# One token sum a slot later, and the last softmax sum taken by TensorE from an unaccumulated unit

## The chip, the cores and the metric

One Trainium2 chip, one core. The metric is device time in microseconds, the median of several executions; lower is better. A profile of one execution of each kernel is at hand.

## What is computed

A transformer block with conditioned norms, in float32, on `x` of shape (4, 1024, 512) with 16 heads of width 32 and a hidden layer of 2048. Cut to what matters:

```python
def norm(x, t, gw, gb, bw, bb):
    g, b = (t @ gw.T + gb)[:, None, :], (t @ bw.T + bb)[:, None, :]
    return g * x * rsqrt(mean(x * x, -1) + 1e-6) + b

def attention(x):                     # q, k, v are projections of x, per head
    p = softmax(einsum('blhd,bmhd->bhlm', q, k) / sqrt(dh))
    return einsum('bhlm,bmhd->blhd', p, v).reshape(B, L, D) @ Wo.T

def swiglu(x):
    return silu(x @ gate_w.T) * (x @ hid_w.T) @ out_w.T

y = x + attention(norm(x, t, g1...))
out = x + y + swiglu(norm(y, t, g2...))
```

## The kernel before

**Tiles.** Activations lie with the features on the partitions. The 4096 tokens are 8 blocks (`n`) of 512; the 512 features are 4 groups (`hg`) of 4 heads. Attention goes by token groups `j` (64 in all: block, head group and half of 256 queries), and each group is 4 units (`r`, 256 in all) of 256 keys. A unit is one tile `raw[r]` of 128 keys x 2 x 4 heads x 256 queries, 1024 KB, from a pool of 10.

**One unit.** `scores` (TensorE, L337), `keep` (ScalarE copies them to `raw`, L344), `running_max` (VectorE, L349), `shifted` (VectorE subtracts the group's maximum, L390), `exponential` (ScalarE, L393), `weighted` (TensorE, `av`, L403) and `accumulate` (L417). The last one gathers the denominators: units 1 to 3 of a group are added into unit 0 by an accumulating DMA that GpSimd (POOL) issues. Each waits for the one before it, since all write the same tile.

**One group.** `fold_sum` (VectorE, L425) adds the two halves of the accumulated tile; `sums` (TensorE, L435, tile `sum`) multiplies by ones to add over the partitions, 4 matmuls; `sums_out` (ScalarE, L440), `inverse` (VectorE, L443) and `normalize` (L452) follow.

**Slots.** The order of PE, DVE, ACT and POOL is written out by hand in a loop over slots `g`: slot `g` issues the scores of unit `g`, the exponential of unit `g - 5`, `av` and the accumulation of unit `g - 6`; every fourth slot (`kind` 0) issues the fold and sums of group `g // 4 - 3`. So the last accumulation (unit 255) stands in slot 261 and the last fold (group 63) in slot 264. SyncE's queue, which issues the plain loads and stores, is ordered by the framework.

**The hidden layer beside it.** From slot 60 on, each two slots also hold one step `p` (128 hidden features for one block, 16 steps per block). Gate and hidden products use a seven-product scheme in the manner of Strassen, on 2 x 2 halves of weights and of tokens. `token_sums(n, i)` makes the sums of token halves for block `n`, in four VectorE instructions on 128x512: T1 (`i = 0`, L518), T2 (`i = 1`, L520), an in-place difference T3 (`i = 2`, L522) and T4 (`i = 3`, L524). T1 is read by `pair_15`, T2 by the right half of `pair_26`, T3 by `pair_7`, T4 by `pair_4`. In an even slot the order around the change is:

```python
scores(g); fold_sum(j_n); shifted(r_x); weighted(r_v); accumulate(r_v); keep(g)
pair_26(p); copy_156(p); take_sums(j_n); exponential(r_x)   # take_sums: sums, sums_out
one(); two()                        # contraction of an earlier step, tile pc
pair_7(p); sub_5(p)
```

and in an odd one `scores`, `shifted`, `weighted`, `keep`, then `pair_3`, `pair_15` of the next step, `add_15` (L551), `gate` (L588), `pair_4` and `hidden` (L591). Work given to `after(g, ...)` is issued at the end of slot `g`. Block `n` begins its hidden layer at slot `g0 + 28`, `g0 = 32 (n + 1)`; that slot has kind 0. For the last block, n = 7, the token sums are issued by a loop of their own behind the slots.

The tiles `sum` and `pc` share a pool of two PSUM banks (tag `w`), and the contraction reads `ow`, 256 KB loaded by SyncE (`load_ow`, L595) a step ahead.

Of the kernel before, what the change touches and what calls it, by code (L numbers as in the profile page):

```python
# [24 lines left out]
def tile_cond_transformer_block(  # L25
# [13 lines left out]
    nc = tc.nc  # L39
# [7 lines left out]
    DH = D // N_HEADS  # L47
    HG = P // DH
# [3 lines left out]
    UN = KT // 2  # L52
# [19 lines left out]
    ones_sum = const.tile([P, DH], F32, tag="ones_sum", name="ones_sum")  # L72
# [45 lines left out]
    raw, rmax, shift, mT, av, acc, avs, oT = {}, {}, {}, {}, {}, {}, {}, {}  # L118
# [16 lines left out]
    def norm_squares(dst, tag: str, k: int):  # L135

        sq = [sb.tile([P, NB], F32, tag="t", name=f"sq{tag}_{2 * k + i}", bufs=2) for i in range(2)]
        for i in range(2):
            nc.scalar.activation(sq[i], dst[:, 2 * k + i, :], AF.Square)
        if k == 0:  # L140
            state[tag] = sb.tile([P, NB], F32, tag="tot", name=f"tot{tag}", bufs=1)
            nc.vector.tensor_tensor(state[tag], sq[0], sq[1], ALU.add)
        else:
            for t in sq:
                nc.vector.tensor_tensor(state[tag], state[tag], t, ALU.add)
# [53 lines left out]
    def norm_scale(dst, tag: str, c: int):  # L199
        nc.vector.tensor_tensor(dst[:, c, :], dst[:, c, :], state[tag], ALU.mult)  # L200

    def norm_mod(which: int, b: int, dst, c: int):
        nc.scalar.activation(  # L203
            dst[:, c, :],
            dst[:, c, :],
            AF.Identity,
            bias=mod[:, (2 * which + 1) * C + c, b : b + 1],
            scale=mod[:, 2 * which * C + c, b : b + 1],
        )
# [201 lines left out]
    def accumulate(r: int):  # L411

        j, u = divmod(r, UN)
        if u == 0:
            acc[j] = raw[r]
        else:
            nc.gpsimd.dma_start(  # L417
                out=acc[j].rearrange("p k h q -> p (k h q)"),
                in_=raw[r].rearrange("p k h q -> p (k h q)"),
                accum_op=ALU.add,  # L420
            )
# [9 lines left out]
    def sums(j: int):  # L431
        total = ps.tile([P, HQ], F32, tag="w", name=f"sum{j}")
        a = acc.pop(j)
        for i in range(HG):
            nc.tensor.matmul(total[i * DH : (i + 1) * DH, :], ones_sum, a[:, 0, i, :], start=True, stop=True)  # L435
        state["sum", j] = total

    def sums_out(j: int):
# [257 lines left out]
    NR = NBLK * C * (NB // HQ) * UN  # L696
# [11 lines left out]
    def pin(g, fn, *a):  # L708
        pinned.setdefault(g, []).append((fn, a))

    def between(g, fn, *a):
        halfway.setdefault(g, []).append((fn, a))

    def after(g, fn, *a):
        ended.setdefault(g, []).append((fn, a))
# [40 lines left out]
    for n in range(NBLK):  # L756
        g0 = (n + 1) * BS
        pin(g0 + 6, load_res, n)
        e = g0 if n == 0 else g0 - 4
        go = e + 13 if n < NBLK - 1 else g0 + 8  # L760
        for d in range(C):
            first.append((go, None, project_out, (n, d)))
            pin(go - 3 + (d // 2 * 4 if n else 0), load_wo, n, d)
        if n < NBLK - 1:
            tag = f"f{n}"
            after(e + 16, add_res, n)
            for k in range(2):
                after(e + 15 + k, lambda n=n, tag=tag, k=k: norm_squares(x2[n], tag, k))
            if n == 0:
                between(e + 17, norm_mean, tag, False)  # L770
            else:
                amid.setdefault(e + 17, []).append((norm_mean, (tag, True)))
            after(e + 17, norm_compact, tag)
            after(e + 19, take, tag)
            after(e + 21, root, tag)
            after(e + 22, invert, tag)
            after(e + 22, put, tag)
            after(e + (23 if n == 0 else 24), norm_spread, tag)
            scales, mods = ((24, 24, 25, 25), (25, 25, 26, 26)) if n == 0 else ((22, 22, 24, 24), (23, 23, 25, 25))
            for c in range(C):  # L780
                after(g0 + scales[c], lambda n=n, tag=tag, c=c: norm_scale(x2[n], tag, c))
                between(g0 + mods[c], lambda n=n, c=c: norm_mod(1, n // QB, x2[n], c))
            for i in range(4):
                after(g0 + (26, 26, 27, 28)[i] - (n > 0 and i == 0), token_sums, n, i)
    for m in range(NBLK * C):
        if m:
            for qh in range(NB // HQ):
# [24 lines left out]
    with tc.manual_schedule(  # L812
# [75 lines left out]
        def take_sums(j: int):  # L888

            if 0 <= j < NR // UN:  # L890
                sums(j)
                sums_out(j)
                if j >= direct:
                    inverse(j)
                    normalize(j)

        while g < END:
# [31 lines left out]
            if v_on:  # L929
                weighted(r_v)  # L930
                accumulate(r_v)
# [120 lines left out]
        n = NBLK - 1  # L1052
# [9 lines left out]
        for i in (1, 3):  # L1062
# [5 lines left out]
                start=True,  # L1068
                stop=True,
# [104 lines left out]
```

## Time and profile before

| | us |
|---|---|
| median of 3 runs | 2425.66 (2425.57 to 2426.95) |
| the profiled execution | 2425.87 |
| its span, first to last instruction | 2424.1 |
| TensorE busy in it | 2374.3 (98%) |
| VectorE busy | 1975.1 (81%) |
| ScalarE busy | 1420.1 (59%) |
| accumulating transfers of `raw` | 192 x 1024 KB, 9.2 median to landing |

Busy TensorE time counts pipelined matmuls by modelled ends. An engine's idle time matters only if another engine's work waits behind it. Times of the profiled execution are compared with its own 2425.87, not with the median.

### The profile page before, as it was taken

To read this page: it belongs to the slowest core of one execution; us is meant where nothing else is said; L and a number is where in the kernel's file an instruction comes from. 1 tells how busy PE (TensorE), PEld (TensorE's weight loads), DVE (VectorE), ACT (ScalarE), POOL (GpSimd) and SP (SyncE) were. 2 spreads that over 40 slices of the span, in tenths; PEclk is the share of its full clock that TensorE was granted. 3 is DMA by queue.
4 is the path that set the end of the run, shared out by engine and by line. 5 is a ranking of instruction groups with operands and counts; after the bars stand their busy time and mean duration, and the time that the engine had idled before them with its cause. 6 is when DMAs were issued, how large, how long until landed. Compare 5 with 4: busy or idle time off the path is not lost. (4 is left out here: it accounts for less than half of the span.)

```text
span 2424.1 us, 74021 instructions
## 1 busy us (share of the span) xinstructions
PE 2374.3 (98%) x33149; PEld 1153.2 (48%) x33149; DVE 1975.1 (81%) x2295; ACT 1420.1 (59%) x1519; POOL 172.4 (7%) x207
## 2 busy tenths in 40 slices
PE   9999999999999999999999999999999999989999
PEld 4333434345454544544454545454545454434665
DVE  2688888889799988998899979997999799835544
ACT  4677776766566656665576657665666576412111
POOL 0000000000000000000000000000000000000000
PEclk9999999999999999999999999999999999999999
DMA  6699999889888888889888888898887988862331
GB/s 226 188 295 254 262 251 241 222 220 239 199 203 212 204 226 199 216 212 229 196 211 217 221 201 213 202 238 202 206 210 197 231 197 219 209 213 82 126 106 53
DMA packets 184843, 499.79 MB, mean 206 GB/s; under 512 B 21191, under 2 KB 78535, under 8 KB 157134
## 3 DMA queue, kind: packets, MB, share of 16 engines
q0 software_dynamic: 28656, 208.68, 44.4%
q1 hardware_dynamic: 155582, 286.37, 35.0%
q8 instruction: 261, 4.28, 0.7%
q14 instruction: 56, 0.46, 0.1%
q10 hardware_dynamic: 288, 0.01, 0.0%
HBM read 244.34 MB, written 41.97 MB: 118 GB/s over the span
## 5 line engine op out<-in xcount | busy, mean ns | idle before, releaser
L390 DVE TENSOR_TENSOR raw<-raw,shift 128x2048 f32<-128x2048 f32 (+1 forms) x320 | 588.8, 1857 | 26.1 <-ACT shift L385 26.1
L344 ACT COPY raw<-sc 128x2048 f32<-128x2048 f32 x256 | 479.4, 1873 | 186.2 <-PE sc L337 127.8
L393 ACT ACTIVATE raw<-raw 128x2048 f32<-128x2048 f32 x256 | 490.7, 1917 | 147.5 <-DVE raw L390 145.3
L349 DVE TENSOR_TENSOR rmax<-rmax,raw 128x1024 f32<-128x1024 f32 x384 | 469.5, 1223 | 47.6 <-ACT raw L344 41.0
L113 PE MATMUL pc<-h,ow 128*32 128x512 f32 x3328 | 379.9, 595 | 2.5 <-ACT raw L393 1.5
L417 POOL DMA_DIRECT2D raw<-raw x192 | 165.3, 861 | 1940.7 <-ACT raw L393 839.0
L337 PE MATMUL sc<-q,k 32*128 32x256 f32 x4096 | 293.3, 400 | 0.8 <-ACT raw L344 0.8
L403 PE MATMUL av<-raw,v 128*32 128x256 f32 x4096 | 272.5, 384 | 21.3 <-ACT raw L393 20.8
L113 PE MATMUL pa<-x,fa 128*32 128x256 f32 x4096 | 270.0, 381 | 3.5 <-DVE pa L551 2.5
L113 PE MATMUL pa<-sums,fw 128*32 128x256 f32 x4096 | 267.9, 379 | 0.0
L337 PEld LDWEIGHTS sc<-q,k 32*128 32x128 f32 x4096 | 185.0, 184 | 117.1 <-issue 74.9
L113 PE MATMUL pkq<-y,wkq 128*32 128x512 f32 (+1 forms) x1664 | 230.8, 596 | 0.9 <-ACT y L203 0.7
L113 PEld LDWEIGHTS pc<-h,ow 128*32 128x32 f32 x3328 | 103.7, 110 | 206.9 <-issue 193.0
L113 PEld LDWEIGHTS pa<-x,fa 128*32 128x32 f32 x4096 | 123.3, 110 | 112.1 <-DVE pa L551 20.9
L113 PEld LDWEIGHTS pa<-sums,fw 128*32 128x32 f32 x4096 | 133.1, 110 | 87.9
L403 PEld LDWEIGHTS av<-raw,v 128*32 128x32 f32 x4096 | 110.6, 109 | 134.5 <-ACT raw L393 48.7
L113 PE MATMUL pb<-x,fw 128*32 128x256 f32 x2048 | 134.7, 379 | 1.2 <-ACT pb L566 1.2
L113 PE MATMUL pa<-x,fw 128*32 128x256 f32 x2048 | 134.0, 379 | 0.0
L113 PE MATMUL pb<-sums,fa 128*32 128x256 f32 x2048 | 133.9, 379 | 0.0
L583 ACT ACTIVATE t<-pa 128x512 f32<-128x512 f32 x128 | 78.3, 612 | 92.9 <-PE pa L113 92.6
L113 PEld LDWEIGHTS pkq<-y,wkq 128*32 128x32 f32 (+1 forms) x1664 | 72.6, 117 | 125.3 <-issue 117.4
L385 ACT COPY shift<-sp 128x512 f32<-128x512 f32 x128 | 75.0, 586 | 95.0 <-PE sp L113 95.0
(132 smaller groups left out, 2338.2 us busy)
## 6 DMA issues: line engine op xcount, KB each, us to landing
raw<-raw POOLq DMA_DIRECT2D x192, 1024.0 KB, 9.2
fw<-sw SPq DMA_DIRECT2D x128, 512.0 KB, 7.3
fa<-in_gh_w SPq DMA_DIRECT2D x128, 384.0 KB, 6.1
ow<-in_out_w SPq DMA_DIRECT2D x104, 256.0 KB, 3.6
wkq<-in_kq_w SPq DMA_DIRECT2D x32, 512.0 KB, 5.8
v<-vs SPq DMA_DIRECT2D x128, 128.0 KB, 6.4
k<-kqs SPq DMA_DIRECT2D x124, 128.0 KB, 6.8
kqs<-st SPq DMA_DIRECT2D x61, 256.0 KB, 8.0
```

The costliest lines, as they stand in the source:

```text
L113: nc.tensor.matmul(dst[k : k + n, :], w[:, k : k + n], moving, start=start, stop=stop, skip_group_check=seeded)
L337: nc.tensor.matmul(sc[:, i, k, :], keys[rows, k * P : (k + 1) * P], queries[rows, :], start=True, stop=True)
L344: nc.scalar.copy(raw[r].rearrange("p k h q -> p h k q"), state.pop(("sc", r)))
L349: nc.vector.tensor_tensor(rmax[j], rmax[j], raw[r][:, k, :, :], ALU.max)
L385: nc.scalar.copy(shift[j][:, k : k + 2, :], pp)
L390: nc.vector.tensor_tensor(t, t, s.unsqueeze(1).to_broadcast(list(t.shape)), ALU.add)
L393: nc.scalar.activation(raw[r], raw[r], AF.Exp)
L403: nc.tensor.matmul(av[j][i * DH : (i + 1) * DH, :], v[m, u][:, k, i * DH : (i + 1) * DH], raw[r][:, k, i, :], start=(kt == 0), stop=(kt == ...
L417: nc.gpsimd.dma_start(out=acc[j].rearrange("p k h q -> p (k h q)"), in_=raw[r].rearrange("p k h q -> p (k h q)"), accum_op=ALU.add,)
L583: nc.scalar.activation(state["t", p], bank_a[p], AF.Tanh, scale=0.5)
```

## The change

Two edits. In `accumulate`, the last unit of all (`r = 255`) is no longer added by a DMA; instead `sums` of its group issues its 4 ones-matmuls three times into the same PSUM tile, first on the folded tile, then on the two halves of `raw[255]` as they are. And T2 is issued at the end of slot `g0 + 27` instead of `g0 + 26` for the blocks n = 1 to 6, where it now stands behind that slot's VectorE work and directly ahead of T3. Block 0 keeps its order.

```diff
@@ accumulate
         if u == 0:
             acc[j] = raw[r]
-        else:
+        elif r < NR - 1:
             nc.gpsimd.dma_start(
                 out=acc[j].rearrange("p k h q -> p (k h q)"),
                 in_=raw[r].rearrange("p k h q -> p (k h q)"),
@@ sums
         a = acc.pop(j)
-        for i in range(HG):
-            nc.tensor.matmul(total[i * DH : (i + 1) * DH, :], ones_sum, a[:, 0, i, :], start=True, stop=True)
+        parts = [a[:, 0]]
+        if (j + 1) * UN == NR:
+            parts += [raw[NR - 1][:, k] for k in range(2)]
+        for k, part in enumerate(parts):
+            for i in range(HG):
+                nc.tensor.matmul(
+                    total[i * DH : (i + 1) * DH, :],
+                    ones_sum,
+                    part[:, i, :],
+                    start=(k == 0),
+                    stop=(k == len(parts) - 1),
+                )
         state["sum", j] = total
@@ the calendar
             for i in range(4):
-                after(g0 + (26, 26, 27, 28)[i] - (n > 0 and i == 0), token_sums, n, i)
+                after(g0 + ((26, 26, 27, 28) if n == 0 else (25, 27, 27, 28))[i], token_sums, n, i)
```

The order of all other instructions on every engine, and of SyncE's queue, is the same in both kernels.

## The prediction

> **What bounds the kernel now.** I read the page's engine shares first, then the waits, then the stretch of the timeline around each place that the change touches. TensorE is busy for 98% of the span, so an edit counts only where it moves the start of a matmul. The idle time at the two places:
>
> ```profile
> PE 2374.3 (98%) x33149; PEld 1153.2 (48%) x33149; DVE 1975.1 (81%) x2295; ACT 1420.1 (59%) x1519; POOL 172.4 (7%) x207
> PE sum L435 <- DVE raw L425: 5.0, 1, 5.0
> DVE raw L425 <- DMA raw<-raw: 5.0, 1, 5.0
> SPq L460 <- DMA ow<-in_out_w: 5.2, 1, 5.2
> ```
>
> Lines two and three are the longest wait of TensorE in the whole trace, and it happens once. The last line (SyncE's own queue, after its issue at 2140.52 us) is used in the rivals. The timeline shows where that wait is: first the last but one token group (j = 62), which has no such wait, then the last one (j = 63). Columns are start, duration, engine, instruction, and in brackets the idle time before it and who ended it.
>
> ```profile
> 2118.66 0.68 DVE L591 TENSOR_TENSOR h<-pb,h 128x512 f32<-128x512 f32 x1
> 2119.26 1.22 DVE L425 TENSOR_TENSOR raw<-raw 128x1024 f32<-128x1024 f32 x1
> 2120.70 0.61 PE L435 MATMUL sum<-raw,ones_sum 128*32 128x256 f32 x8
> 2121.80 3.64 PE L113 MATMUL pc<-h,ow 128*32 128x512 f32 x32 [0.49 <-ACT total L440]
> 2125.26 1.05 PE L113 MATMUL pb<-x,fw 128*32 128x256 f32 x16
> ...
> 2135.24 0.86 POOL L417 DMA_DIRECT2D raw<-raw  x1 [10.83 <-DMA raw<-raw]
> 2140.53 0.69 DVE L591 TENSOR_TENSOR h<-pb,h 128x512 f32<-128x512 f32 x1
> 2141.50 1.04 PE L113 MATMUL pa<-sums,fw 128*32 128x256 f32 x16
> 2146.20 1.23 DVE L425 TENSOR_TENSOR raw<-raw 128x1024 f32<-128x1024 f32 x1 [4.98 <-DMA raw<-raw]
> 2147.53 0.90 PE L435 MATMUL sum<-raw,ones_sum 128*32 128x256 f32 x8 [4.98 <-DVE raw L425]
> 2148.89 4.75 PE L113 MATMUL pc<-h,ow 128*32 128x512 f32 x32 [0.47 <-ACT total L440]
> 2153.47 0.82 PE L113 MATMUL pb<-x,fw 128*32 128x256 f32 x12
> ```
>
> The accumulating transfer of unit 255 can only be issued at 2135.24, because POOL waits until the one of unit 254 has landed. It lands at 2146.2, `fold_sum` waits for it, and TensorE waits for `fold_sum`. After the gap the same 32 contraction matmuls take 4.75 us and not 3.64, and `sum` takes 0.90 and not 0.61. The stage view says why (columns: stretch, length, PE busy, granted clock, DMA share, GB/s); the clock was 1.00 before and after this stretch:
>
> ```profile
> 2147.77:2151.18 3.41, 2.94 (x20) 0.50 0.67 267
> ```
>
> For the other edit I read the change of blocks at n = 1. The first lines are VectorE from T2 to the fold, the last ones TensorE in the same time:
>
> ```profile
> 773.45 0.68 DVE L520 TENSOR_TENSOR sums<-x,sums 128x512 f32<-128x512 f32 x1
> 774.05 2.29 DVE L390 TENSOR_TENSOR raw<-raw,shift 128x2048 f32<-128x2048 f32 x1
> 780.05 0.68 DVE L522 TENSOR_TENSOR x<-x 128x512 f32<-128x512 f32 x1
> 780.65 1.22 DVE L425 TENSOR_TENSOR raw<-raw 128x1024 f32<-128x1024 f32 x1
> 778.34 1.07 PE L403 MATMUL av<-raw,v 128*32 128x256 f32 x16 [1.20 <-ACT raw L393]
> 780.49 1.05 PE L113 MATMUL pa<-sums,fw 128*32 128x256 f32 x16
> 781.98 0.64 PE L435 MATMUL sum<-raw,ones_sum 128*32 128x256 f32 x8 [0.44 <-PE pa L113]
> ```
>
> The reader is to see two TensorE waits. One is 1.20 us before `av`: T2 stands ahead of `shifted` (L390) on VectorE, which feeds the exponential, which feeds `av`. The other is before `sum`. Its bracket names PE, but the fold ends at 780.65 + 1.22 = 781.87 and `sum` starts 0.11 us later; the plain handover at j = 63 is 2147.53 - (2146.20 + 1.23) = 0.10 us. So `sum` waits for the fold. The stage view gives VectorE 8.42 us busy in the 8.42 us from 773.45 to 781.87: there is no hole in it.
>
> **Part 1: the last unit's transfer goes.** Removed: one POOL issue (0.86 us, the last on its queue, nothing behind it) and 1024 KB of accumulation. Added: 8 matmuls of 128x256 and a longer live range of `raw[255]`. Step by step:
>
> The fold now depends on the transfer of unit 254, which had landed by 2135.24 (it is what POOL waited for). So the fold follows L591 in VectorE's order: at j = 62 it starts 2119.26 - 2118.66 = 0.60 us after it, so now at 2140.53 + 0.60 = 2141.13, and ends at 2142.35. With the handover of 0.10, `sum` can start at 2142.45. TensorE itself is free at 2141.50 + 0.87 = 2142.37 (0.87 is 2120.70 less 2119.83, the same pair's start, at j = 62), so the wait left is about 0.1 us.
>
> The 8 new matmuls are not in the trace. The nearest row is `av` (L403): also 8 matmuls, 16 records, of the same shape, and the next group starts 0.86 us after it. The lower end is 0.86 (two times 0.43 for `sum`'s 8 records at full rate); the upper end is 1.7, if the clock were halved. I take 0.86. Their operand is long ready: the exponential of unit 255 ended at 2124.6.
>
> At j = 62 the contraction starts 2121.80 - 2120.70 = 1.10 us after `sum`. So now it starts at 2142.45 + 1.10 + 0.86 = 2144.41, against 2148.89: 4.48 us earlier. At full clock it takes 2125.26 - 2121.80 = 3.46 us up to the next group, against 2153.47 - 2148.89 = 4.58: another 1.12 us. Sum: 5.60 us. TensorE then runs without a gap until 2208, so the shift is not used up; later waits there (1.20 at 2209.5, 1.49 at 2229.3) are for ScalarE and VectorE work that moves along with it. VectorE's reciprocal and `normalize`, 2.2 us, still end ahead of the output projection (2151.1 against 2156.9 before).
>
> Two rules bear on this. **First**, the transfer's price. The trace has 9.2 us as the median landing of these 1024 KB and 10.9 us here. The Trainium skill ("DMA: Bandwidth & Descriptors", section "Anatomy of one DMA — SWDGE (gpsimd) path") gives about 2.0 us plus the bytes over 436 GB/s, an estimate of 4.4 us. By the rule it would have landed at 2135.24 + 4.4 = 2139.6, before the fold's turn at 2141.13; the transfer would be hidden, and the change would only cost 0.86 us. The measured wait of 4.98 us decides. **Second**, the clock. The skill ("TensorE: Matmul & The Clock Gate", section "Part 1: The HAM clock gate") says that an idle window of some 3.4 us halves the clock for at least another such window, and prices it at half the throttled time: 1.71 us. The rows give 1.12 on the contraction and 0.29 on `sum` (already in the 4.48). By the rule for all of it the gain would be 4.48 - 0.29 + 1.71 = 5.9; I take 5.60 from the rows.
>
> **Part 2: T2 one slot later, six blocks (n = 1 to 6).** Nothing is added or removed on any queue; 0.60 us of VectorE time (start to start) moves from ahead of `shifted` to ahead of T3 (L522). So `shifted`, the exponential, `av`, `add_15` and the left half of `pair_26` each come 0.60 us earlier. A new wait appears: the right half of `pair_26` reads T2, which now ends near 780.13, so it starts at 780.2 instead of 780.49, about 0.3 us after TensorE would be ready. Queued behind it is `sum`. But `sum` waits for the fold, and VectorE's work up to the fold is the same without a hole, so `sum` still starts at 781.98. The 0.60 us won before `av` come back as wait before `sum`. Worth: 0 per block. Bounds per block: a gain of 0.60 if `sum` did not wait for the fold (six times: 3.6), a loss of 0.3 if the new wait were not covered (1.8). I take 0, since all six blocks show VectorE just as full.
>
> **Sum.** 2425.87 (the profiled execution, 1.8 us more than its span) less 5.60 is 2420.27; that execution lies 0.2 above the median of the runs, so I say 2420.1.
>
> **Rivals.** (a) T2 gains as well: 2416.5. For it: the 1.20 us wait is real. Against it: the fold's time. Chance 0.06. (b) The wait changes its owner: the contraction reads `ow`, a 256 KB load behind the same transfer. SyncE's next issue waited 5.2 us for it from 2141.2, so it landed near 2146.4, after the new start of 2144.41. If it still landed then, the contraction would start at 2146.45 and gain only 2.44, or 3.6 with the clock kept: 2422.1 to 2423.2. Against it: the transfer that held the loads back is gone, and at the 389 GB/s of that stretch 256 KB take 0.7 us. Chance 0.09. (c) Slower: the clock halves at the block changes. It did so after the stretch at 130.5 to 133.9, when TensorE was busy 1.49 of 3.41 us; it did not at 2.02 of 3.41 (777.14 to 780.55). Should the shifted gaps push a window below about 1.5 busy, each of the six blocks loses the 1.41 us seen above, 8.5 in all: 2428.6. By my new times the worst window is busy 2.3, so 0.03. (d) Small new waits take back 1 to 2 us: 2421.1 to 2422.1, chance 0.06. The rest, 0.76, is the forecast, between 2419.3 and 2421.
>
> **Numbers.** Range 2418.6 to 2422.6: the likeliest case, (d), and the nearer end of (b). A measurement of this kernel can tell about 0.2%, 4.85 us, from no change; the forecast of 5.6 is beyond that by little. Faster by more: most of the likeliest case and (a), 0.73. Within: the rest of it, (b), (d) and (c), 0.24. Slower by more: 0.03.
>
> **What would show it.** Right: one L417 fewer; no wait of 5 us before the last L425 and L435; 24 records of `sum` there (its line is L439 in the changed kernel); the contraction after it in 3.6 us at clock 1.00; at the block changes `av` 0.6 us earlier and `sum` at the same distance from T1 as before (16.8 us). Wrong: a wait of the last contraction for `ow`; `sum` earlier at the block changes; a clock of 0.50 there.

## The result

The changed kernel takes 2419.27 us (median of 10 runs, 2418.27 to 2420.85), the kernel before 2425.61 (10 runs, 2423.88 to 2428.27). The ratio is 0.9974, 95% interval 0.9965 to 0.9984: some 6.3 us faster, with 3.9 to 8.5 in the interval. The profiled execution takes 2419.99 us, span 2418.2, which is 5.9 less than its counterpart before. The forecast was 2420.1, in a range of 2418.6 to 2422.6.

The last token group in the timeline of the changed kernel (start, duration, engine, instruction, idle before it), and the same stretch after `sum` in the stage view (stretch, length, PE busy, granted clock, DMA share, GB/s). `sum` is at L439 there:

```profile
2140.86 1.22 DVE L425 TENSOR_TENSOR raw<-raw 128x1024 f32<-128x1024 f32 x1
2142.18 1.50 PE L439 MATMUL sum<-raw,ones_sum 128*32 128x256 f32 x24
2144.16 3.64 PE L113 MATMUL pc<-h,ow 128*32 128x512 f32 x32 [0.48 <-ACT total L450]
2147.62 1.05 PE L113 MATMUL pb<-x,fw 128*32 128x256 f32 x16
2144.16:2147.57 3.41, 3.41 (x32) 1.00 0.12 45
```

The fold has no bracket any more: it follows VectorE's own queue. The contraction takes 3.64 us and not 4.75, at clock 1.00. As a yardstick that doesn't depend on what came earlier, take the time from the start of the tanh of step 101, in slot 263, to `pair_7` behind the last contraction (the `pb` line). The tanh before, then in the changed kernel:

```profile
2138.00 0.60 ACT L583 ACTIVATE t<-pa 128x512 f32<-128x512 f32 x1 [4.86 <-PE pa L113]
2137.72 0.60 ACT L593 ACTIVATE t<-pa 128x512 f32<-128x512 f32 x1 [4.86 <-PE pa L113]
```

Before, the yardstick is 2153.47 - 2138.00 = 15.47 us, now 2147.62 - 2137.72 = 9.90: the last group gives 5.57 us. From there to the end both traces take the same time (270.6 us).

The change of blocks at n = 1: T1 before and in the changed kernel, then of the changed kernel VectorE, TensorE, and the stage row up to the end of the fold (stretch, length, busy time of PE, PEld, DVE, ACT and POOL, granted clock, DMA share, GB/s):

```profile
765.20 0.68 DVE L518 TENSOR_TENSOR sums<-x 128x512 f32<-128x512 f32 x1
765.00 0.68 DVE L528 TENSOR_TENSOR sums<-x 128x512 f32<-128x512 f32 x1
773.26 2.28 DVE L390 TENSOR_TENSOR raw<-raw,shift 128x2048 f32<-128x2048 f32 x1
779.26 0.68 DVE L530 TENSOR_TENSOR sums<-x,sums 128x512 f32<-128x512 f32 x1
780.46 1.22 DVE L425 TENSOR_TENSOR raw<-raw 128x1024 f32<-128x1024 f32 x1
777.53 1.07 PE L403 MATMUL av<-raw,v 128*32 128x256 f32 x16 [0.60 <-ACT raw L393]
779.99 1.07 PE L113 MATMUL pa<-sums,fw 128*32 128x256 f32 x16
781.77 0.64 PE L439 MATMUL sum<-raw,ones_sum 128*32 128x256 f32 x8 [0.71 <-PE pa L113]
773.26:781.68 8.42, 6.88 (x112) 3.28 (x104) 8.42 (x11) 4.60 (x5) 0.86 (x1) 1.00 1.03 265
```

The wait before `av` has shrunk from 1.20 to 0.60 us, and the one before `sum` has grown from 0.44 to 0.71. The other 0.3 us went before the right half of `pair_26` (the line at 779.99), which now waits for T2. From T1 to `sum` it is 16.77 us, as before, and the same to 0.01 us in all six blocks.

### The profile page after: what moved, and what is told of

It reads as the page before. It is cut to its first block, busy times and chain, and to the rows that moved or that the text cites. A ratio compares the mean times of both kernels' runs of the same rounds, so it can differ in the third digit from the quotient of the medians.

```text
span 2418.2 us, 74050 instructions
## 1 busy us (share of the span) xinstructions
PE 2373.7 (98%) x33165; PEld 1152.5 (48%) x33165; DVE 1974.4 (82%) x2295; ACT 1421.2 (59%) x1519; POOL 171.7 (7%) x206
```

## The experiments

The theory on trial: the whole gain comes from the last group, through the wait and the clock after it; T2's move is worth nothing, because the fold sets `sum`. The rivals: T2 has a share; or the wait alone is not the cost, and the loads behind the transfer matter.

**T2 alone.**

```diff
-                after(g0 + (26, 26, 27, 28)[i] - (n > 0 and i == 0), token_sums, n, i)
+                after(g0 + ((26, 26, 27, 28) if n == 0 else (25, 27, 27, 28))[i], token_sums, n, i)
```

> Only T2 moves; the last unit is accumulated by its transfer as before. My theory (T2's 0.60 us move inside a stretch of VectorE without a hole, and the fold at its end sets the next matmul): no change, within 0.3 us of the kernel before in the profiled stretch from T1 of block 1 to the last fold, and the 5 us wait before the last fold stays. Rival (T2 wins its 0.60 us six times): 3.6 us faster, with `sum` after each block change 0.6 us earlier counted from T1.

Measured: ratio 1.0003 (0.9994 to 1.0012), medians 2425.97 against 2425.16. From T1 to `sum` it is 16.77 us in all six blocks, and from T1 of block 1 to T1 of block 6 it is 1280.65 us against 1280.71. Over these five blocks T2's move is worth less than 0.1 us. The wait before the last fold is there again, and this execution shows more; the timeline and the stage view (stretch, length, PE busy, granted clock, DMA share, GB/s):

```profile
2144.83 1.23 DVE L425 TENSOR_TENSOR raw<-raw 128x1024 f32<-128x1024 f32 x1 [4.72 <-DMA raw<-raw]
2147.72 5.93 PE L113 MATMUL pc<-h,ow 128*32 128x512 f32 x32 [0.48 <-ACT total L440]
2145.64:2149.05 3.41, 2.41 (x16) 0.50 0.99 392
2149.05:2152.46 3.41, 3.41 (x20) 0.51 0.07 27
```

Here the clock is halved for two stretches of 3.41 us, not one, and the contraction takes 5.93 us. The yardstick is 2153.48 - 2136.89 = 16.59, so 1.12 us more than in the kernel before, for a wait that was 0.26 us shorter. In the first throttled stretch TensorE was idle for about 1 us (busy 2.41 of 3.41), in the single one of the kernel before for 0.47 (2.94 of 3.41). That this decides whether a second one follows is suggested by these two traces, not shown.

**The last unit alone.** The two edits in `accumulate` and `sums`, with T2 in its old place:

```diff
+        elif r < NR - 1:
...
+            parts += [raw[NR - 1][:, k] for k in range(2)]
```

> Only the last unit's sum goes to TensorE; T2 stays where it was. My theory: the whole gain is here, 5.6 us, with the contraction after the last `sum` taking 3.6 us at clock 1.00. Rival (T2 has a share): 2 us, or the difference to the changed kernel's median, 6.3 us, is shared between this and the other half.

Measured: ratio 0.9970 (0.9959 to 0.9981), median 2418.36. The two ends of the yardstick, and the contraction:

```profile
2136.07 0.60 ACT L593 ACTIVATE t<-pa 128x512 f32<-128x512 f32 x1 [4.86 <-PE pa L113]
2142.50 3.64 PE L113 MATMUL pc<-h,ow 128*32 128x512 f32 x32 [0.48 <-ACT total L450]
2145.96 1.05 PE L113 MATMUL pb<-x,fw 128*32 128x256 f32 x16
```

It is 2145.96 - 2136.07 = 9.89 us, against 9.90 with both edits. This half makes the whole gain; the rival that T2 has a share has fallen.

**The transfer back, with nobody waiting for it.** Two accumulating transfers of 512 KB, from the last unit into two tiles that nothing reads any more. POOL issues them when the transfer of unit 254 has landed; the two small copies on ScalarE carry that dependence.

```diff
+    def unawaited(j: int):
+        for t, k in ((shift[j], 0), (rmax[j], 1)):
+            nc.scalar.copy(t[:, 0, 0:1], acc[j][:, 0, 0, 0:1])
+            nc.gpsimd.dma_start(
+                out=t.rearrange("p h q -> p (h q)"),
+                in_=raw[NR - 1][:, k].rearrange("p h q -> p (h q)"),
+                accum_op=ALU.add,
+            )
...
+    after(NR + 6, unawaited, NR // UN - 1)
```

> The changed kernel with the transfer's traffic put back and nobody waiting for it: two accumulating transfers of 512 KB each, from the last unit into two dead tiles, issued by POOL when the transfer of unit 254 has landed (two 1-element ScalarE copies carry that dependence). If the wait alone cost the time: the gain of the changed kernel stays, within 0.5 us. Rival (the loads behind the transfer are late): the contraction after the last `sum` waits for its 256 KB of weights to about 2146 us, the clock halves, and 2.5 to 4.5 us of the gain are lost again.

Measured: ratio 0.9994 (0.9985 to 1.0003), median 2423.59. In the timeline, and last in SyncE's waits (total, times, longest):

```profile
2132.97 0.86 POOL L426 DMA_DIRECT2D shift<-raw  x1 [9.26 <-ACT rmax L425]
2133.50 1.21 POOL L426 DMA_DIRECT2D rmax<-raw  x1
2141.18 1.50 PE L448 MATMUL sum<-raw,ones_sum 128*32 128x256 f32 x24
2145.73 5.34 PE L113 MATMUL pc<-h,ow 128*32 128x512 f32 x32 [3.05 <-DMA ow<-in_out_w]
SPq L479 <- DMA ow<-in_out_w: 6.0, 1, 6.0
```

`sum` comes as early as in the changed kernel. But the contraction behind it now waits for its 256 KB of weights, issued by SyncE at 2134.20 and landed about 2145.7, and then runs at half clock (0.50 from 2145.93 to 2149.34). The yardstick is 2150.86 - 2136.73 = 14.13: of the 5.57 us only 1.34 are left. So these two transfers cost 4.2 us although nothing waits for their sum. They are a stand-in for the old transfer, not the same: the weights landed some 9.0 us after the tanh here, and some 8.4 in the kernel before (SyncE's wait ended near 2146.4). By that difference, an estimate, the old transfer left unwaited would have cost some 0.6 us less. This is the rival (b) of the prediction. In the changed kernel it doesn't act: SyncE waits only 0.4 us for the same weights, so they landed near 2141.0, 3 us ahead of the contraction.

**The wait kept, TensorE kept busy.**

```diff
+        if (j + 1) * UN == NR:
+            for _ in range(10):
+                nc.tensor.matmul(
+                    total.rearrange("p (a c) -> p a c", a=QT),
+                    ones_mean,
+                    ones_mean.unsqueeze(1).to_broadcast([P, QT, P]),
+                    start=True,
+                    stop=True,
+                )
```

> The kernel before, with ten 128x256 matmuls of a constant into the tile `sum` ahead of its last use, so that TensorE works through the 5 us wait; their result is overwritten. About 0.43 us each, 4.3 us in all, they end before the transfer lands. If the clock was the reason for the slow contraction after the wait: clock 1.00 there, contraction 3.6 instead of 4.75 us, `sum` 0.6 instead of 0.9, 1.4 us faster than the kernel before. If the slow contraction had another reason (its weights or PSUM): no change.

Measured: ratio 0.9995 (0.9987 to 1.0004), medians 2424.32 against 2425.16, which tells nothing alone. The timeline does:

```profile
2141.01 4.58 PE L436 MATMUL sum<-ones_mean 128*128 128x256 f32 x20
2145.82 0.64 PE L444 MATMUL sum<-raw,ones_sum 128*32 128x256 f32 x8 [0.23 <-DVE raw L425]
2146.95 3.64 PE L113 MATMUL pc<-h,ow 128*32 128x512 f32 x32 [0.49 <-ACT total L449]
```

With the same wait for the transfer, but TensorE at work in it, the contraction is back at 3.64 us, and the clock stays at 1.00 from 2141.00 to 2150.40. The yardstick is 2150.41 - 2136.53 = 13.88, so 1.59 us less than before. Of these 0.19 come from a transfer that landed a little earlier (fold 8.01 us after the tanh, 8.20 before). The contraction gives 1.12 (4.58 to 3.46 up to `pair_7`), and the way from `sum` to the contraction 0.23 (1.36 to 1.13); the last 0.05 lie between the fold and `sum`, with no cause shown. So the clock is 1.35 to 1.40 us of the 5.57, and the wait, less the added matmuls, the rest.

**T3 behind the fold.** If the fold is what sets `sum`, work must be taken from ahead of it. T3 needs to be done only by `pair_7`, later in that slot:

```diff
+                if n and i == 2:
+                    behind.setdefault(g0 + 28, []).append((token_sums, (n, i)))
+                    continue
...
             if x_on and kind != 1:
                 shifted(r_x)
+            for fn, a in behind.pop(g, []):
+                fn(*a)
```

> The changed kernel, and T3 moved as well, in blocks 1 to 6: from the end of slot g0 + 27 to behind the fold and `shifted` of slot g0 + 28, still ahead of `pair_7`, its reader. My theory says that T2's move was worth nothing because the fold, not T2, sets `sum`, and VectorE has no hole up to the fold. So taking 0.60 us of work from ahead of the fold must start `sum` 0.60 us earlier after each block change (16.17 us after T1 instead of 16.77), 3.6 us in all, about 2416 against 2419.3 of the changed kernel. Rival (`sum` waits for TensorE's own order, as the bracket in the trace says): no change.

Measured: ratio 0.9968 (0.9955 to 0.9980), median 2418.58. TensorE, then VectorE:

```profile
781.37 0.64 PE L439 MATMUL sum<-raw,ones_sum 128*32 128x256 f32 x8
787.83 0.27 PE L374 MATMUL pt<-ident_bf,split 128*32 128x128 bf16 x2 [0.36 <-DVE res L614]
785.95 1.22 DVE L352 TENSOR_TENSOR rmax<-raw 128x1024 f32<-128x1024 f32 x1
787.09 0.68 DVE L614 SCALAR_TENSOR_TENSOR res<-pc,res 128x512 f32<-128x512 f32 x1
```

`sum` comes 781.37 - 765.20 = 16.17 us after T1, 0.60 earlier, in all six blocks: the fold does set it, whatever the bracket said. But each block gains only 0.2 us (T1 to the next T1 255.88 us, 256.07 in the changed kernel). VectorE is still full up to L614 (`take_contract`), which frees the bank that `pt` writes, and `pt` now waits for it. The expectation of 3.6 us was too high: it ended at `sum` and did not ask what would be late next. Between blocks 5 and 6 this execution lost 0.8 us again (256.86 us): the fold at 1894.89 us waited 1.49 us for its accumulating transfer. In the kernel before that fold waited 0.59 us, at no cost to TensorE.

**The same with T2 in its old place.**

```diff
-                after(g0 + ((26, 26, 27, 28) if n == 0 else (25, 27, 27, 28))[i], token_sums, n, i)
+                after(g0 + ((26, 26, 27, 28) if n == 0 else (25, 26, 27, 28))[i], token_sums, n, i)
```

> As the kernel with T3 behind the fold, but T2 in its old place, at the end of slot g0 + 26. My theory: VectorE's work up to the fold is the same in both orders, so `sum` comes as early as there, and the times agree within 0.3 us in the profiled stretch. Rival (T2's move pays once the fold is out of the way): up to 0.3 us per block slower than that kernel, 1.8 in all, because the right half of `pair_26` ends 0.5 us later and then sets `sum`.

Measured: ratio 0.9965 (0.9952 to 0.9977), median 2417.78. `sum` is again 16.17 us behind T1 in all six blocks, and each block gains the same 0.2 us, now in all five intervals. T2's place is indifferent here too.

**Two units as they are.**

```diff
-        elif r < NR - 1:
+        elif r < NR - 2:
...
-            parts += [raw[NR - 1][:, k] for k in range(2)]
+            parts += [raw[r][:, k] for r in (NR - 2, NR - 1) for k in range(2)]
```

> The changed kernel, but the last two units go to TensorE as they are (20 matmuls in the last `sum`, one accumulating transfer fewer). Measures the price of 8 matmuls where no transfer is waited for: 0.86 us slower than the changed kernel in the profiled stretch from the last fold to the contraction, and nothing gained, since the transfer of unit 254 had landed 5 us before the fold's turn. Rival (loads behind that transfer matter): a wait elsewhere goes and some of it comes back.

Measured: ratio 0.9974 (0.9963 to 0.9984), median 2420.11.

```profile
2139.40 2.37 PE L439 MATMUL sum<-raw,ones_sum 128*32 128x256 f32 x40
```

`sum` has 40 records now, and the yardstick is 2145.70 - 2134.94 = 10.76, so 0.86 us more than with 24. Eight such matmuls cost 0.86 us, and the transfer of unit 254, which nobody had been waiting for, gives nothing back.

**The first maximum behind `take_contract`.** The T3 kernel, and in those six slots:

```diff
-                if g < NR:
+                if g < NR and not turned:
                     running_max(g, 0)
                     running_max(g, 1)
...
                 pair_7(p)
                 sub_5(p)
+                if turned:
+                    running_max(g, 0)
+                    running_max(g, 1)
```

> The kernel with T3 behind the fold kept only 0.2 of the 0.6 us per block: `sum` came 0.60 us earlier, but the transposes `pt` then waited 0.36 us for VectorE's L614 (`take_contract`), which frees the PSUM bank and stands behind the first maximum of the next group (L352, 1.22 us). Here that maximum is issued behind `take_contract` and `sub_5` in those six slots. If VectorE's queue was the reason: `pt` no longer waits there, some 0.36 us more per block, so 0.55 us per block against the changed kernel, 3.3 us in all. If the bank was free and `pt` waited for its own operand: nothing more.

Measured: ratio 0.9961 (0.9948 to 0.9973), median 2415.59. TensorE, then VectorE, in the same place:

```profile
779.97 0.64 PE L439 MATMUL sum<-raw,ones_sum 128*32 128x256 f32 x8
786.02 0.27 PE L374 MATMUL pt<-ident_bf,split 128*32 128x128 bf16 x2
785.28 0.69 DVE L614 SCALAR_TENSOR_TENSOR res<-pc,res 128x512 f32<-128x512 f32 x1 [0.63 <-PE pc L113]
786.55 1.22 DVE L352 TENSOR_TENSOR rmax<-raw 128x1024 f32<-128x1024 f32 x1
```

`pt` no longer waits, L614 waits for TensorE and not the other way round, and each block now gains 0.60 us: 3.6 us in all up to the tanh of step 101. In this execution 1.0 us of it is lost again at the last group (yardstick 10.87), where TensorE waits 0.78 us for the load of `fa`. By the medians this version beats both kernels.

**The changed kernel again**, unaltered, beside the last version.

> The changed kernel once more, on the same chip as the last version, to compare the two directly and to see how much its start differs from run to run. About 2419.3; the stretch from the first block change to the end within 0.3 us of its first profile.

Measured: ratio 0.9977 (0.9968 to 0.9986), median 2419.47. So the last version is 3.9 us faster by the medians of runs taken side by side (2414.51 to 2417.09 against 2418.18 to 2421.03). The stretch from T1 of block 1 to the end agrees with the first profile to 0.2 us. The start does not: the exponential of unit 72 comes at 669.71 us here and at 670.62 in the first profile of the same kernel. The granted clock tells most of why. Here it is 0.50 from 11.4 to 14.8 us, in the first profile from 132.6 to 136.0, each time for 3.41 us. The earlier one delays unit 0 by 0.84 us (86.08 against 85.24). From the exponential of unit 0 to that of unit 14 it takes 112.12 to 112.15 us in the five traces with the later throttled stretch and 110.43 to 110.46 in the six without: 1.69 us for one stretch through which TensorE was busy. Together that is 0.85 of the 0.91.

## Why the prediction was right

- **The fold moves up to VectorE's own turn.** Forecast 0.60 us behind L591, 2141.13; measured 2140.86, also 0.60 behind it (2140.26). The other 0.27 were won ahead of the last group.
- **The eight matmuls.** Forecast 0.86, by the `av` row. `sum` starts 1.98 us ahead of the contraction, with 1.10 + 0.86 forecast, and the kernel with two units measured 0.86 by itself.
- **The clock.** Forecast 1.12 on the contraction and 0.29 on `sum`, 1.41; the kernel that kept TensorE busy measured 1.12 and 0.23, and 0.05 that can't be placed. The 0.29 compares lengths of `sum`; from its start to the contraction the prediction's own rows give 1.36 - 1.10 = 0.26, and only that is in its sum. The rule's estimate of 1.71 was too high for the stretch after the wait, of which TensorE idled 0.47 us; where TensorE was busy throughout, at 133 us, 1.69 were lost. With two throttled stretches it took 8.64 us from the fold to `pair_7`, against 7.27 with one: 1.37 more.
- **The sum.** Forecast 5.60, measured 5.57 on the yardstick, and 5.58 with T2 left alone. It was worked out from an execution with one throttled stretch after the wait; that another can have two was not in it.
- **The price of the transfer.** The rule's estimate would have made it hidden. The transfer that was kept in the T2 kernel held the fold back by 4.72 us, so the measured row was right to decide.
- **T2 is worth nothing.** Shown from both sides: moving T2 alone left `sum` at 16.77 us behind T1, and taking T3 from ahead of the fold brought it to 16.17. The new wait was forecast too: the right half of `pair_26` comes 14.99 us after T1, forecast 15.00.
- **Rival (b)** was given 0.09 and did not happen. The reason given against it, that the traffic goes with the wait, is what the unawaited transfers showed: with the traffic back, the contraction waited 3.05 us for `ow`. The figure beside that reason was too low: 256 KB in 0.7 us by the bandwidth, but even in the changed kernel `ow` landed some 6 us after its issue (2135.01 to about 2141.0), in time all the same.
- **Rivals (a), (c) and (d)** did not happen: no gain at T2, no halved clock at a block change, no new wait of more than 0.2 us behind the last `sum`. For (c), the stretch from 777.14 us is not one of those in which the clock is set (see the last section); in those at the block changes TensorE is busy for 2.2 of 3.41 us or more before and 2.7 in the changed kernel, well above the 1.49.
- **What is left.** The medians differ by 6.3 us and the profiled stretch by 5.6. The granted clock of the runs gives an estimate of the rest. Its mean is 0.99782 over 56 runs of the kernel before and 0.99895 over 20 of the changed kernel. One stretch of 3.41 us at half clock takes 1.71 of some 2420 us, 0.0007, so the kernel before has some 1.6 stretches more (1.1 to 2.1 by the scatter; 1.3 on the one chip for which both are on record), if those elsewhere come equally often in both. If one always follows the wait, as in both traces in which TensorE idled through it, a second comes in roughly half of the executions, at 1.37 us each. That is about the 0.7 us that is missing, but the interval is wide, and no run counts the stretches one by one. Between single profiles the start adds up to 1 us either way: the throttled stretches at 11 and 133 us, and a wait near 587 us that is not set by the edits (2.52 us in the changed kernel, 1.53 in the version with two units, which has both).

## What to carry to other kernels

Work moved within a full stretch of an engine gained nothing here, because the instruction at its end set the next matmul. So ask which instruction ends the full stretch (here the fold, then `take_contract`), and move work from ahead of that one to behind it. A transfer at the end of a pipeline can be paid for twice, by who waits for its data and by the loads queued behind its traffic; with the wait gone and such traffic left, a quarter of this gain remained. When TensorE idles for some microseconds, look at the granted clock behind the gap and add the slow matmuls to its price, here 1.4 us on a wait of 5, and 2.8 where a second stretch was throttled.

## What the runs showed of the hardware

- A 256 KB load issued behind two accumulating transfers of 512 KB each landed some 11.5 us after its issue (2134.20 to about 2145.7). Loads of the same size landed in 2.5 us in a quieter stretch of the kernel before.
- After nearly the same wait (4.98 and 4.72 us) the clock was halved for 3.4 us in one execution and for 6.8 in another.
- Throttled stretches lie on a fixed grid within a trace. In the kernel before they start at 11.03, 133.91 and 2147.77 us, which are 36 and 590 times 3.413 us apart. On that grid, from 20 us on and in all eleven traces, the clock halved after every stretch at full clock in which TensorE was busy (by modelled ends) for 1.53 of 3.41 us or less, and after none with 1.65 or more. In between it went both ways: 1.59 us was followed by a halved clock in one trace and not in another. The halving near 11 us, after a stretch that counts as busy, doesn't fit this.
